# Two additions moved from VectorE to TensorE and ScalarE, and TensorE's ration counted anew, in a Mamba and linear-attention kernel

## The chip, the cores and the metric

The kernel runs on one core of a Trainium2 chip. The metric is the device time of one execution in microseconds (us), as the median of several runs. A profile of one execution comes with it. The engines are named PE or TensorE (matrix products; PEld is its loading of weights), DVE or VectorE, ACT or ScalarE, POOL or GpSimd, and SP, which here only issues DMAs. Each engine takes its instructions in the order in which they were written to it.

## The reference

The input x has 4 batches of 512 channels on 64 x 64 places; flattened, 4096 time steps. Two layers follow each other, and each adds its input to its output.

```python
# layer 0: x = x + L0(group_norm(x))
xn = layer_norm(xf)                                  # over the 512 channels
chunks = xn in 4 chunks of 128 channels, each a sequence of its own
xz = chunks @ in_proj_w.T;  xi, z = split(xz)        # 256 channels each
xc = silu(conv4(xi) + conv_b)                        # causal, 4 taps, by channel
dt, Bs, Cs = xc @ x_proj_w.T;  dt = softplus(dt @ dt_proj_w.T + dt_proj_b)
h = exp(dt * A) * h + (dt * xc) * B                  # 16 states for each channel
y = sum over states of h * C;  y = (y + xc * D_param) * silu(z)
ym = y @ out_proj_w.T + skip_scale * chunks          # the skip addition
out = layer_norm(ym) @ proj_w.T + proj_b             # then x + out: the input addition
# layer 1: x = x + L1(group_norm(x)): linear attention, 8 heads, ReLU on q and k,
# then an output projection
```

## The kernel before

**Tiles and steps.** Time is cut into 8 tiles of 512. A step is one chunk (128 channels) of one tile of one batch: 4 x 8 x 4 = 128 steps, c innermost. Each step's recurrence takes 16 slots. A slot holds two scans of 128 x 512 on VectorE (`slot`, L582, the scan at L596), where the partitions are 32 channels times 4 states. Around the scans stand: the decay exp(dt A) on ScalarE into one of two PSUM buffers (`decay`, L565), dt x B on GpSimd (`drive`, L574), two slots ahead into three buffers, the product with C (`product`, L614), whose first 384 columns are VectorE's, from a bank c_all that TensorE spreads (`c_row`, L559), and whose last 128 columns are GpSimd's (L607), and the sum over the states, on TensorE with the constant `fold` (`fold_states`, L625). The matrix `fold` is four 32 x 32 identities under each other.

**What else runs in the slots.** The function `after` (L971) is called at the end of each slot and hands out the rest of the work at fixed slots s of the step: gate on GpSimd (s = 1 and 9), the softplus of the next step (s = 2), the output product of the step before (`out_proj`, L647, s = 3) and its skip addition on VectorE (`with_skip`, L652, s = 5), the inputs of the step after next (`inputs`, L440), Silu (s = 10), and so on. At s = 2 and 10 (`AWAY`) ScalarE is away with table loads.

**The queues of generators.** Four lists hold work that is handed out piece by piece: `ahead` (group norm and layer norm of the next tile), `late` (`projected`, L409: the second layer norm, the projection and the input addition of a finished tile), `rest` (`attention`, L668, of the batch before) and `light` (`stats0`, L656: the statistics of the next batch, two pieces of VectorE work for a tile of x at the AWAY slots). A piece that yields "wait" is tried again. `later(n, what)` puts an instruction off by n slots, so that its operands are there. `work_bank` takes one of four PSUM banks; `load` takes one of three tiles of x and issues its DMA on SP.

**The ration.** `mm` (L117) counts each product in `work["mm"]`, in units of a 128 x 512 fp32 product (a quarter for bf16; for products that run abreast, their share). In each slot, a credit of 2.5 units less what `after` itself issued decides whether a queue may issue products:

```python
credit = min(credit + 2.5 - (work["mm"] - start), 2.5)
```

Here `start` is taken at the top of `after`, so the products of `fold_states` and `c_row`, which `slot` issues before it, are not counted.

**The end.** The attention of a batch needs the whole batch's first layer. That of batches 0 to 2 runs in the slots of the next batch; that of batch 3 runs after the last scan, with no recurrence beside it.

Of the kernel before, what the change touches and what calls it, by code (L numbers as in the profile page):

```python
# [11 lines left out]
ALU = mybir.AluOpType  # L12
# [12 lines left out]
def kernel(  # L25
# [53 lines left out]
    def work_bank(name, behind=1):  # L79
        held[0] += behind  # L80
        return ps_w.tile([P, T], F32, tag="w", name=name)

    def free(n=1):
        held[0] -= n
# [15 lines left out]
    def until(*done):  # L100
        while not all(done):
            yield "wait"
# [92 lines left out]
    def column(v, n, name):  # L195
        t = const.tile([P, n], F32, tag=name, name=name)
        nc.scalar.dma_start(t, v.rearrange("(c p) -> p c", p=P))
        return t

    def rows(v, t, queue=nc.scalar):  # L200
        queue.dma_start(t, v.rearrange("(c p) f -> p c f", p=P))
        return t
# [39 lines left out]
        nc.vector.tensor_scalar(dg[:, e, :], ident, dpar[:, e : e + 1], None, ALU.mult)  # L242
    g_sb = column(norm_g, NC, "g_sb")
    b_sb = column(norm_b, NC, "b_sb")
    a_sb = rows(a_log, wk.tile([P, NH, NST], F32, tag="sq", name="a_sb", bufs=4))
    w_op = const_rows(op_w, "w_op")
    sk = const.tile([P, 1], F32, tag="sk", name="sk")
# [22 lines left out]
    for k in range(KS):  # L270
        for j in range(NJ):
            nc.sync.dma_start(
                a_t[k * BLK : (k + 1) * BLK, :, j, :], a_k[j * BLK : (j + 1) * BLK, :, k, :]
            )

    for o in range(NC):
        pw = work_bank(f"pw_{o}")
# [131 lines left out]
    def projected(ym, stats, x1, b, t):  # L409

        nm = f"{b}_{t}"
        yield from layer_norm(ym, f"b_{nm}", False)
        xt = yield from load_x(b, t, "r")
        taken = []

        def take(o, pp):
            nc.vector.scalar_tensor_tensor(  # L417
                xt[:, o, :], pp, pb[:, o : o + 1], xt[:, o, :], ALU.add, ALU.add
            )
            nc.vector.bn_stats(stats[:, o, t, :], xt[:, o, :])  # L420
            free()

        for o in range(NC):
            yield from room()
            pp = work_bank(f"pp_{nm}_{o}")
            for c in range(NC):
                mm(
                    pp, w_pr[:, c, o * P : (o + 1) * P], ym[:, c, :],
                    start=(c == 0), stop=(c == NC - 1),
                )  # L430
                if c == 1:
                    yield "more"
            taken.append(later(2, lambda o=o, pp=pp: take(o, pp)))
            yield
        yield from until(*taken)
        nc.sync.dma_start(x1, xt)
        later(2, free_x)

# [205 lines left out]
            f["xz"][:, 1, e, :], f["xz"][:, 1, e, :], f["xz"][:, 0, e, :], ALU.mult  # L644
        )

    def out_proj(f, nm):  # L647
        f["po"] = work_bank(f"po_{nm}", 0)
        for e in range(NH):
            mm(f["po"], w_op[:, e, :], f["xz"][:, 1, e, :], start=(e == 0), stop=(e == NH - 1))  # L650

    def with_skip(f, xn, c):  # L652
        v = xn[:, c, NTAP - 1 : NTAP - 1 + T]
        nc.vector.scalar_tensor_tensor(v, v, sk, f["po"], ALU.mult, ALU.add)

    def stats0(stats, b):  # L656

        for t in range(NT):
            xt = yield from load_x(b, t, "s")
            yield  # L660
            for c in range(NC):
                nc.vector.bn_stats(stats[:, c, t, :], xt[:, c, :])
                if c == NC - 1:
                    later(1, free_x)
                if c % 2:
                    yield

    def attention(b, x1s, stats):  # L668

# [165 lines left out]
        free_x()  # L835
        free_x()
        for o in range(NC):
            r = slice(o * P, (o + 1) * P)
            nc.vector.tensor_tensor(m3[:, o, r], m3[:, o, r], ident, ALU.add)
        def store(t, o, pp):  # L840
            res = wk.tile([P, T], F32, tag="res", name=f"res_{b}_{t}_{o}", bufs=1)
            nc.scalar.activation(res, pp, AF.Identity, bias=ob[:, o : o + 1])
# [112 lines left out]
        decay(k)  # L955

    with tc.manual_schedule():
        credit, mix, held[0], held_x[0] = 0.0, iter(()), 0, 0
        for n, (b, t, c) in enumerate(steps):
            f, nm = fs[n], names[n]  # L960
            before = fs[n - 1] if n else None
            nxt = fs[n + 1] if n + 1 < N else None
            front = step_inputs(n + 2) if n + 2 < N else iter(())
            last_mix, mix = mix, mixers(fs[n + 2], names[n + 2]) if n + 2 < N else iter(())
            if c == 0 and (t + 1 < NT or b + 1 < B):
                add_to(ahead, tile_norm(b, t + 1) if t + 1 < NT else tile_norm(b + 1, 0))
            if c == 0 and t == 0 and b + 1 < B:
                add_to(light, input_norm(b + 1))
            assert c != 2 or not ahead
            for s in range(SLOTS):  # L970
                def after():  # L971
                    nonlocal credit
                    start = work["mm"]
                    now[0] = n * SLOTS + s
                    for what in [w for at, w in due if at <= now[0]]:
                        what()
                    due[:] = [d for d in due if d[0] > now[0]]
                    if s == 0 and before is not None:
                        take_y(before, n - 1, 1)
                    if s == SLOTS // 2:  # L980
                        take_y(f, n, 0)
                    if s < 2:
                        next(last_mix, None)
                    if s == 1:
                        spread(f, 1, nm)
                        if before is not None:
                            gate(before, 1)
                        if nxt is not None:
                            time_banks(nxt, names[n + 1])
                    if s == 2 and nxt is not None:  # L990
                        nc.scalar.preload_act_table_set("softplus")
                        time_steps(nxt, names[n + 1])
                        nc.scalar.preload_act_table_set("natural_log_exp_and_others")
                    if s == 5 and before is not None:
                        pb_, pt_, pc_ = steps[n - 1]
                        with_skip(before, xn[pb_, pt_], pc_)
                        if pc_ == NC - 1:
                            add_to(late, leave(pb_, pt_))
                    if s in (2, 4, 5, 6, 7, 8):
                        next(front, None)  # L1000
                    if s == 3 and nxt is not None:
                        to_rows(nxt, 0, names[n + 1])
                        to_rows(nxt, 1, names[n + 1])
                    if s == 3 and before is not None:
                        out_proj(before, names[n - 1])
                    if s == 9:
                        gate(f, 0)
                        if nxt is not None:
                            spread(nxt, 0, names[n + 1])
                    if s == 10 and n + 2 < N:  # L1010
                        silu(n + 2)
                        nc.scalar.preload_act_table_set("natural_log_exp_and_others")
                    if s >= 12:
                        next(mix, None)
                    may = [
                        what for k, what in ((0, "wide"), (1, "one ahead"), (2, "two ahead"))
                        if any(a - 2 * k <= s <= a - k for a in AWAY) or (k == 2 and s >= SLOTS - 2)
                    ]
                    if s in AWAY and not any(q and q[0][1] == "wide" for q in (ahead, late)):
                        one(light)  # L1020

                    limit[0] = 3 if 9 <= s < 13 else 2
                    credit = min(credit + 2.5 - (work["mm"] - start), 2.5)
                    busy = False
                    for queue in (ahead, late, rest):
                        kind = queue[0][1] if queue else None
                        if queue is ahead or kind == "free" or credit > 0 or kind == "more" and not busy:
                            start = work["mm"]
                            one(queue, ANYWHERE if queue is ahead and (c, s) > (1, 4) else may)
                            credit -= work["mm"] - start  # L1030
                            busy = busy or work["mm"] - start > 1

                slot(n * SLOTS + s, N * SLOTS, after)
            fs[n - 1].clear() if n else None
        product(N * SLOTS - 1, N * SLOTS)
        now[0] = None
        for _, what in due:
            what()
    take_y(fs[N - 1], N - 1, 1)
    gate(fs[N - 1], 1)  # L1040
    out_proj(fs[N - 1], names[N - 1])
    with_skip(fs[N - 1], xn[B - 1, NT - 1], NC - 1)
    add_to(late, leave(B - 1, NT - 1))
    while late or rest:
# [54 lines left out]
```

## Time and profile before

| | us |
|---|---|
| median of 3 runs | 8307.17 (8304.55 to 8308.64) |
| the profiled execution | 8301.55 |
| its span | 8299.8 |
| first scan, end of the last product of the recurrence | 122.8, 7845.5 |
| busy: VectorE, GpSimd, TensorE, ScalarE | 7350.8, 6856.9, 6564.5, 5235.9 |
| DMA | 153 GB/s on average |

A group of the profile is read so: the line of the kernel, the engine, the operation, the tile written and the tiles read with their shapes, the count; then the busy time and the mean duration in ns; then the idle time of the engine just before these instructions and what ended it. A row of the waits reads: who waited, for whom, us in total, how many times, the longest. Every product on TensorE has line 120, that of the helper `mm`, so there one goes by the names of the tiles: po is the output product, pp the projection, pq, pk and pr the attention's products, y the sum over the states, pc the taps. A product of fp32 operands leaves two records.

### The profile page before, as it was taken

To read this page: it belongs to the slowest core of one execution; us is meant where nothing else is said; L and a number is where in the kernel's file an instruction comes from. 1 tells how busy PE (TensorE), PEld (TensorE's weight loads), DVE (VectorE), ACT (ScalarE), POOL (GpSimd) and SP (SyncE) were. 2 spreads that over 40 slices of the span, in tenths; PEclk is the share of its full clock that TensorE was granted. 3 is DMA by queue.
4 is the path that set the end of the run, shared out by engine and by line. 5 is a ranking of instruction groups with operands and counts; after the bars stand their busy time and mean duration, and the time that the engine had idled before them with its cause. 6 is when DMAs were issued, how large, how long until landed. Compare 5 with 4: busy or idle time off the path is not lost. (4 is left out here: it accounts for less than half of the span.)

```text
span 8299.8 us, 86977 instructions
## 1 busy us (share of the span) xinstructions
PE 6564.5 (79%) x22240; PEld 2203.5 (27%) x22240; DVE 7350.8 (89%) x7097; ACT 5235.9 (63%) x7585; POOL 6856.9 (83%) x4565
## 2 busy tenths in 40 slices
PE   5667676667788878788788888788788888888699
PEld 1111121112222222222222222223222222232244
DVE  5999999999999999989999999999999999999700
ACT  4666666666666666666677666666666666666421
POOL 4999999999888888888898888888988888888600
PEclk8787888777889989899898999889889999889799
DMA  5666666556666565666666666657666655666412
GB/s 158 160 157 153 152 158 151 146 143 158 161 161 154 144 162 148 159 180 172 168 152 159 161 154 160 154 151 190 161 160 157 152 147 144 154 168 177 128 41 86
DMA packets 829306, 1266.15 MB, mean 153 GB/s; under 512 B 183920, under 2 KB 317568, under 8 KB 816512
## 3 DMA queue, kind: packets, MB, share of 16 engines
q1 hardware_dynamic: 821632, 1255.87, 59.6%
q10 hardware_dynamic: 7168, 4.71, 0.2%
q8 instruction: 174, 2.85, 0.2%
q14 instruction: 332, 2.72, 0.1%
HBM read 1053.28 MB, written 206.57 MB: 152 GB/s over the span
## 5 line engine op out<-in xcount | busy, mean ns | idle before, releaser
L578 POOL TENSOR_TENSOR bx<-d_all,b_all 128x1024 f32<-128x1024 f32 x2048 | 4795.3, 2362 | 107.3 <-DVE h L596 90.4
L596 DVE TENSOR_TENSOR_SCAN h<-dA,st,bx 128x512 f32<-128x512 f32 x3584 | 4448.5, 1272 | 228.2 <-ACT dA L570 182.8
L570 ACT ACTIVATE dA<-d_all,a_t 128x512 f32<-128x512 f32 x4096 | 2805.3, 689 | 2473.2 <-DVE h L596 2450.5
L619 DVE TENSOR_TENSOR h<-h,c_all 128x768 f32<-128x768 f32 x2048 | 1913.7, 934 | 91.3 <-PE c_all L120 81.3
L120 PE MATMUL y<-h,fold 128*32 128x512 f32 x8192 | 1329.7, 727 | 128.2 <-POOL h L607 121.9
L120 PE MATMUL c_all<-parts,sel 128*128 128x384 bf16 x1024 | 379.6, 371 | 1316.0 <-DVE h L619 1313.4
L607 POOL TENSOR_TENSOR h<-h,c_sb 128x512 f32<-128x512 f32 x1024 | 1298.9, 1268 | 129.8 <-DMA c_sb<-c_rows 28.5
L120 PE MATMUL pq<-w_qk,xa 128*128 128x512 f32 x2048 | 1038.9, 639 | 1.1 <-ACT xa L321 1.1
L120 PE MATMUL pc<-xn,w_cv 128*128 128x512 f32 x2048 | 1026.8, 631 | 11.3 <-ACT xn L389 4.6
L606 POOL COPY st<-h 128x4 f32<-128x4 f32 x1024 | 193.3, 189 | 640.4 <-DVE h L596 580.0
L120 PEld LDWEIGHTS <-sel 128*128 128x128 bf16 x1280 | 128.1, 100 | 2133.0 <-DVE h L619 1933.8
L596 DVE TENSOR_TENSOR_SCAN h<-dA,bx 128x512 f32<-128x512 f32 x512 | 604.2, 1211 | 87.0 <-ACT dA L570 83.4
L120 PEld LDWEIGHTS pc<-xn,w_cv 128*128 128x128 f32 x2048 | 382.3, 199 | 674.3 <-issue 559.7
L120 PEld LDWEIGHTS pq<-w_qk,xa 128*128 128x128 f32 x2048 | 413.1, 206 | 491.1 <-issue 471.7
L120 PE MATMUL pp<-xn,w_pr 128*128 128x512 f32 x1024 | 523.9, 642 | 3.8 <-DVE xn L383 3.8
L120 PE MATMUL pr<-xb,m 128*128 128x512 f32 x1024 | 514.9, 641 | 2.7 <-ACT xz L469 2.3
L120 PE MATMUL pt<-dt,w_dt 32*128 32x512 f32 x512 | 276.0, 879 | 116.7 <-ACT parts L525 50.6
L120 PE MATMUL y<-xz,dg 128*128 128x512 f32 x512 | 347.9, 769 | 0.0
L120 PEld LDWEIGHTS y<-h,fold 128*32 128x32 f32 x8192 | 172.4, 116 | 651.3 <-issue 310.8
L643 POOL TENSOR_TENSOR xz<-xz 128x512 f32<-128x512 f32 x256 | 325.3, 1271 | 2.7 <-ACT xz L640 2.7
L488 POOL TENSOR_TENSOR dt<-dt,xz 128x1024 f32<-128x1024 f32 x128 | 302.8, 2366 | 20.5 <-ACT dt L481 20.5
L120 PE MATMUL pd<-xz,w_xp 128*128 128x512 f32 x512 | 297.0, 710 | 7.8 <-ACT xz L911 7.8
(151 smaller groups left out, 5871.3 us busy)
## 6 DMA issues: line engine op xcount, KB each, us to landing
d_all<-d_rows SPq DMA_DIRECT2D x2048, 256.0 KB, 6.5
b_all<-b_rows SPq DMA_DIRECT2D x4096, 64.0 KB, 2.1
d_rows<-dt SPq DMA_DIRECT2D x256, 512.0 KB, 3.0
c_sb<-c_rows SPq DMA_DIRECT2D x4096, 16.0 KB, 1.8
xs<-in_x_dram SPq DMA_DIRECT2D x32, 1024.0 KB, 7.3
xn<-in_x_dram SPq DMA_DIRECT2D x32, 1024.0 KB, 6.1
xr<-in_x_dram SPq DMA_DIRECT2D x32, 1024.0 KB, 6.4
x<-xr SPq DMA_DIRECT2D x32, 1024.0 KB, 4.0
```

The costliest lines, as they stand in the source:

```text
L120: nc.tensor.matmul(out_, lhsT, rhs, **how)
L488: nc.gpsimd.tensor_tensor(f["both"][:, 1], f["both"][:, 0], f["xz"][:, 0], ALU.mult)
L570: nc.scalar.activation(dAs[k], fs[n]["d_all", e][:, 0, j, :], AF.Exp, scale=a_t[:, e, j, q : q + 1])
L578: nc.gpsimd.tensor_tensor(bxs[g], fs[n]["d_all", e][:, 1, jj * 2 : jj * 2 + 2, :], bc(b_all[g // JJ], 2), ALU.mult)
L596: nc.vector.tensor_tensor_scan(h[:, j, :], dAs.pop(2 * g + i), bxs[g][:, i, :], 0.0 if t == 0 else st[:, c, e, q, j : j + 1], ALU.mult, AL ...
L606: nc.gpsimd.tensor_copy(st[:, c, e, q, :], h[:, :, T - 1])
L607: nc.gpsimd.tensor_tensor(h[:, :, CUT:], h[:, :, CUT:], bc(c_sb.pop(g // JJ), NJ), ALU.mult)
L619: nc.vector.tensor_tensor(own, own, bc(c_all[g // JJ], 2), ALU.mult)
L643: nc.gpsimd.tensor_tensor(f["xz"][:, 1, e, :], f["xz"][:, 1, e, :], f["xz"][:, 0, e, :], ALU.mult)
```

## The change

The skip addition becomes a product: `out_proj` first multiplies the chunk with `skd`, a diagonal matrix of the skip scale, into the bank po, and the two products of the output projection are added to it there. `with_skip` is then a copy from the bank, on ScalarE. The input addition becomes four products of 32 x 32 blocks of `fold` with the tile xr, added to the bank pp; ScalarE takes the bank out with the bias, and the statistics of the result (`bn_stats`) follow one slot later, as does the store. `skd` takes the place of `ident` in memory, so that the later addition of the identity to m3 goes by blocks of `fold`. A tile of `stats0` is loaded in the slot after the last tile's work, not at the next AWAY slot. The credit is now 3.5 units a slot, at most 2.6, and `seen` makes it count all products since the last slot, those of the recurrence too.

```diff
+    skd = ident
...
+    nc.vector.tensor_scalar(skd, ident, sk, None, ALU.mult)
...
         def take(o, pp):
-            nc.vector.scalar_tensor_tensor(
-                xt[:, o, :], pp, pb[:, o : o + 1], xt[:, o, :], ALU.add, ALU.add
-            )
-            nc.vector.bn_stats(stats[:, o, t, :], xt[:, o, :])
+            nc.scalar.activation(xt[:, o, :], pp, AF.Identity, bias=pb[:, o : o + 1])
             free()
+            later(1, lambda: nc.vector.bn_stats(stats[:, o, t, :], xt[:, o, :]))
...
                 mm(
                     pp, w_pr[:, c, o * P : (o + 1) * P], ym[:, c, :],
-                    start=(c == 0), stop=(c == NC - 1),
+                    start=(c == 0), stop=False,
                 )
                 if c == 1:
                     yield "more"
+            for k in range(P // BLK):
+                r = slice(k * BLK, (k + 1) * BLK)
+                mm(pp[r, :], fold[r, :], xt[r, o, :], abreast=P // BLK, start=False, stop=True)
             taken.append(later(2, lambda o=o, pp=pp: take(o, pp)))
             yield
         yield from until(*taken)
+        yield from pause(1)
         nc.sync.dma_start(x1, xt)
...
-    def out_proj(f, nm):
-        f["po"] = work_bank(f"po_{nm}", 0)
+    def out_proj(f, xn, c, nm):
+        po = f["po"] = work_bank(f"po_{nm}", 0)
+        mm(po, skd, xn[:, c, NTAP - 1 : NTAP - 1 + T], start=True, stop=False)
         for e in range(NH):
-            mm(f["po"], w_op[:, e, :], f["xz"][:, 1, e, :], start=(e == 0), stop=(e == NH - 1))
+            mm(po, w_op[:, e, :], f["xz"][:, 1, e, :], start=False, stop=(e == NH - 1))
...
-        v = xn[:, c, NTAP - 1 : NTAP - 1 + T]
-        nc.vector.scalar_tensor_tensor(v, v, sk, f["po"], ALU.mult, ALU.add)
+        nc.scalar.copy(xn[:, c, NTAP - 1 : NTAP - 1 + T], f["po"])
...
-                    yield
+                    yield "wait" if c == NC - 1 else None
...
         for o in range(NC):
-            r = slice(o * P, (o + 1) * P)
-            nc.vector.tensor_tensor(m3[:, o, r], m3[:, o, r], ident, ALU.add)
+            for k in range(P // BLK):
+                r = slice(k * BLK, (k + 1) * BLK)
+                v = m3[r, o, o * P + k * BLK : o * P + (k + 1) * BLK]
+                nc.vector.tensor_tensor(v, v, fold[r, :], ALU.add)
...
-                    start = work["mm"]
...
-                    if s in AWAY and not any(q and q[0][1] == "wide" for q in (ahead, late)):
+                    if light and light[0][1] == "wait" or s in AWAY and not any(
+                        q and q[0][1] == "wide" for q in (ahead, late)
+                    ):
                         one(light)
...
-                    credit = min(credit + 2.5 - (work["mm"] - start), 2.5)
+                    credit = min(credit + 3.5 - (work["mm"] - seen), 2.6)
...
+                    seen = work["mm"]
```

More of the change, by code (lines that the diff above doesn't have):

```diff
@@ L957 @@
     with tc.manual_schedule():
-        credit, mix, held[0], held_x[0] = 0.0, iter(()), 0, 0
+        credit, seen, mix, held[0], held_x[0] = 0.0, work["mm"], iter(()), 0, 0
         for n, (b, t, c) in enumerate(steps):
@@ L971, in after @@
                 def after():
-                    nonlocal credit
-                    start = work["mm"]
+                    nonlocal credit, seen
                     now[0] = n * SLOTS + s
@@ L1004, in after @@
                     if s == 3 and before is not None:
-                        out_proj(before, names[n - 1])
+                        pb_, pt_, pc_ = steps[n - 1]
+                        out_proj(before, xn[pb_, pt_], pc_, names[n - 1])
                     if s == 9:
@@ L1040 @@
     gate(fs[N - 1], 1)
-    out_proj(fs[N - 1], names[N - 1])
+    out_proj(fs[N - 1], xn[B - 1, NT - 1], NC - 1, names[N - 1])
     with_skip(fs[N - 1], xn[B - 1, NT - 1], NC - 1)
```

## The prediction

> **What bounds the kernel now.** I read the busy line first, then the costliest groups, then the stretches of the span, then the waits of VectorE, and last the chain of waits for the end.
>
> ```profile
> PE 6564.5 (79%) x22240; PEld 2203.5 (27%) x22240; DVE 7350.8 (89%) x7097; ACT 5235.9 (63%) x7585; POOL 6856.9 (83%) x4565
> ...
> L596 DVE TENSOR_TENSOR_SCAN h<-dA,st,bx 128x512 f32<-128x512 f32 x3584 | 4448.5, 1272 | 228.2 <-ACT dA L570 182.8
> ...
> L619 DVE TENSOR_TENSOR h<-h,c_all 128x768 f32<-128x768 f32 x2048 | 1913.7, 934 | 91.3 <-PE c_all L120 81.3
> ```
>
> VectorE leads, with two scans and one product in each slot (2 x 1.272 + 0.934 = 3.48 us). The share over the whole span hides that there are two stages. The rows of the stretches show them (each engine: busy us, then its instructions in brackets; after POOL the granted clock):
>
> ```profile
> 200.00:2110.00 1910.00, 1324.09 (x4155) 370.35 (x4156) 1844.81 (x1740) 1258.38 (x1803) 1755.04 (x1169) 0.79 0.62 153
> 2110.00:4020.00 1910.00, 1557.37 (x5434) 530.21 (x5432) 1784.60 (x1717) 1265.57 (x1838) 1661.76 (x1106) 0.91 0.63 161
> ...
> 7900.00:8300.00 400.00, 392.98 (x1436) 183.32 (x1434) 16.86 (x45) 83.03 (x129) 0.00 (x0) 0.98 0.17 61
> ```
>
> The recurrence runs from the first scan at 122.8 to the end of the last at 7844.5: 7722 us, 128 steps of 16 slots, 3.77 us a slot. In batch 0 (first row) VectorE is busy 97% of the time; once the attention of the batch before runs beside it (second row) 93%, with TensorE at 82%. In all it idles 437 us of the 7640 between 200 and 7840. The last row is the tail: the last batch's attention, TensorE alone at 98%. The chain of waits holds nearly only this tail (PE pq, pr), so it says nothing of the stage in which the change lies. What VectorE waits for:
>
> ```profile
> DVE h L596 <- ACT dA L570: 266.3, 178, 49.1
> ...
> DVE h L619 <- PE c_all L120: 81.3, 63, 3.0
> ...
> DVE xn L654 <- PE po L120: 16.8, 16, 6.8
> DVE xr L417 <- PE pp L120: 15.8, 8, 6.4
> ```
>
> The first comes at ScalarE's table loads and Silu, which the change leaves alone. The second is TensorE's queue running late. All 63 of those waits lie where attention runs, none in batch 0.
>
> **What the Trainium skill says.** "VectorE: DVE Perf Modes", Specifications, puts VectorE closer to SBUF and ScalarE closer to PSUM; here ScalarE's copy of a 128x512 bank takes 0.578 us (L469) and VectorE's addition out of one 0.729 us (L654), which agrees. "TensorE: Matmul & The Clock Gate", Part 1, says that idling throttles the clock and activity releases it; the granted clock is 0.79 in batch 0 and 0.91 with attention, so added products should not slow the others. Part 3 of that page says products on distinct row groups of the array run abreast; two K=32 products (pt, four records) took 1.13 us together at 2469.40, as long as one full product. It also says that matmuls start and end in order. So a product that waits for a DMA holds all behind it.
>
> **The change, part by part.**
>
> *VectorE's work removed.* The rows are:
>
> ```profile
> L417 DVE SCALAR_TENSOR_TENSOR xr<-pp,pb,xr 128x512 f32<-128x512 f32 x128 | 94.0, 735 | 48.5 <-PE pp L120 15.8 <-DMA b_all<-b_rows 14.6 <-DMA xr<-in_x_dram 12.1
> L654 DVE SCALAR_TENSOR_TENSOR xn<-xn,sk,po 128x512 f32<-128x512 f32 x128 | 93.3, 729 | 17.3 <-PE po L120 16.8
> ```
>
> 127 of the L654 lie in the recurrence (the last step's is in the tail) and 124 of the L417 (the last tile's four are in the tail): 127 x 0.729 + 124 x 0.735 = 183.7 us, on an engine 94% busy: **-184**.
>
> *Waits of VectorE removed.* Idle before those rows was 17.3 and 48.5; in the tail 6.8 and 11.0; so 48 us in the recurrence. What they waited for (products, and xr landing) is still waited for, by ScalarE and TensorE. I take half as gained: **-24** (0 to -48).
>
> *ScalarE's pieces.* 127 copies (0.58) and 124 Identity with a bias (0.68, as L842): 158 us on an engine 63% busy, with no table load (Identity already stands among the Exp at L453). What can suffer is the decay (L570) queued behind a piece. In the timeline ScalarE idles alternately 0.48 and 1.35 us before each decay, and a decay takes 0.69 where the next scan takes 1.28 before it is needed. So a piece in the short gap makes the decay some 0.2 late, inside that slack; two pieces together, or one beside a table load, cost. I take 0.1 each: **+25** (0 to +158). A piece also holds the queue when TensorE is late with its bank: that was VectorE's wait above.
>
> *TensorE's products.* Each step gets a skip product (po: 260.8 us for 256 products of two records, 1.02 each) and each tile four groups of four 32x32 products abreast; the like group (y, eight records) runs in 1.06 when nothing holds it. 128 x 1.02 + 128 x 1.06 = 266 us more on an engine that has 18% free beside attention. Cost comes through c_all: its product stands behind the slot's other products, and VectorE waits. I counted the products between one c_all and the next in the order of both programs (in units of a 128x512 fp32 product; bf16 and 32-wide ones a quarter). A unit takes 0.86 when dense (two products every 1.72 us at 3036.85), 0.94 at a clock of 0.91, so a pair of slots (7.54 us) holds about 8. Pairs over 8 units: 163 before, 229 after. The c_all waits (81.3 before L619, 6.6 before L596) times 229/163 give **+36** (-30, if the evener ration spreads them, to +200, priced below).
>
> *The fold products wait for the load of xr.* In batch 0 they stand one slot behind it:
>
> ```profile
> 475.56 1.01 SPq L130 DMA_DIRECT2D xr<-in_x_dram  x1
> ...
> 479.09 1.88 PE L120 MATMUL pp<-xn,w_pr 128*128 128x512 f32 x4
> ...
> 483.81 0.75 DVE L417 SCALAR_TENSOR_TENSOR xr<-pp,pb,xr 128x512 f32<-128x512 f32 x1 [2.18 <-DMA xr<-in_x_dram]
> ```
>
> TensorE would stand from 480.97 to about 483.8, some 2.8 us, with two tap products (pc, 1.72) and the next c_all behind it: 483.8 + 1.06 + 1.72 + 0.32 = 486.9, where VectorE wants it at 486.39. VectorE lost 2.18 to this load before, so this is an exchange, and I count nothing more. In batches 1 to 3 most tiles have about three slots (11 us) between their first product and the fold in the written-out order; the longest landing was 11.8. If that cover goes, it is 2.8 x 31 tiles = 87 on TensorE.
>
> *GpSimd.* It idles 869 us between 200 and 7840, 6.8 a step; VectorE gets 1.44 a step faster (183.7/128). Most of GpSimd's waits are for the scan, and its bursts (gate, dt) must be caught up in less time: **+15** (0 to +92).
>
> *The ration.* Limit 3.5 with the recurrence's own work (0.72 units a slot: 1.0 fold, 0.19 c_all, a quarter of 1.0 for y, per pair) is 2.78 for the rest against 2.5. The order of the changed program shows what that yields: the attentions' last products stand at steps 64.7, 96.7 and 126.75 of 128, before at 64.4, 96.4 and 126.9. None spills into the tail, so **0** of itself (its spreading is in the -30 above).
>
> *The rest.* The earlier loads of xs move DMAs on SP's queue by some slots; the bn_stats behind them are as many, at the same slots: 0, and if a tile is then short the attention would end late, which the order excludes. The store of xr goes one slot later; it is read a batch later: 0. The 16 additions of ident (0.785) become 64 of 32x32, near the fold copies' 0.172 (L188): 12.6 against 11.0, 0. The extra scaling of ident is 0.28 at the start. The tail gets one skip product and four groups in its serial part: **+5** (3 to 8).
>
> Sum: -184 - 24 + 25 + 36 + 15 + 5 = **-127**. The profiled execution took 8301.55 (span 8299.8): 8174.6. The median of the runs, 8307.17, is 5.6 above it, so **8180**.
>
> **The rivals.**
>
> *TensorE becomes the bound (slower).* With attention beside it, every added product passes on to c_all and to VectorE: 96 steps x (1.02 + 1.06) = 200 in place of 36, so -184 - 24 + 25 + 200 + 15 + 5 = +37: 8344. It decides where VectorE's waits for c_all go from 88 to over 88 + 163 = 251. For: 82% busy, 20 waits a batch already, pairs over 10 units 54 before and 82 after. Against: the mean pair goes only from 6.0 to 6.2 units, and every pair below 8 catches up what one above it left. 0.14.
>
> *ScalarE's pieces land in full.* 158 in place of 25: +6, 8313, no change. For: the decay is what VectorE waits for most. Against: those waits cluster at table loads, and pieces like L453 run now without a wait beside them. 0.08.
>
> *GpSimd takes over half.* It gives back 92: -50, 8257. For: 89% busy in the recurrence. Against: VectorE waits only 11 us for it now (bx, h, st). 0.10.
>
> *The change does not do what it says.* The ration might be all that acts; the order above speaks against it, and the removed rows are gone from VectorE's order.
>
> **How the numbers follow.** The forecast has 0.68, its own range is 8095 (-212: waits all gone, ScalarE's pieces free, c_all no worse) to 8260 (about 60 for ScalarE's pieces and 70 for c_all). With the rivals the range goes to 8315, which leaves out the slower case (0.14) and about 0.05 below. 0.2%, 17 us, is about what a measurement of this kernel can tell from no change: faster 0.68 + 0.10 = 0.78, same 0.08, slower 0.14.
>
> **What would show it.** Right: VectorE busy near 7164, its idle between 200 and the last scan near 490 (437 - 24 + 25 + 36 + 15), c_all waits near 125, no VectorE row for po or pp; TensorE busy near 6830; the tail 5 longer. Wrong: c_all waits above 250, waits for dA grown by over 100, GpSimd's idle unchanged while VectorE's grows, or po or fold rows well over 1.1 us a group.

## The result, and the profile after

The changed kernel takes 8273.33 us (median of 4 runs, 8265.77 to 8280.80) against 8305.86 (4 runs, 8303.44 to 8308.64) for the kernel before on the same chip: a ratio of 0.9961, 95% interval 0.9943 to 0.9978. It gains 33 us, 0.4%, where 127 were forecast. The direction was right, the size was not: the range held the time, but the likeliest value is 93 us off. The profiled execution took 8270.61 us, with a span of 8268.9. The granted clock hardly differs: where attention runs it is 0.92 (0.91 before).

The page's busy line and the two groups that carry the recurrence:

```profile
PE 6698.2 (81%) x23450; PEld 2248.1 (27%) x23520; DVE 7187.9 (87%) x6890; ACT 5366.3 (65%) x7841; POOL 6856.1 (83%) x4565
...
L602 DVE TENSOR_TENSOR_SCAN h<-dA,st,bx 128x512 f32<-128x512 f32 x3584 | 4432.6, 1269 | 236.4 <-ACT dA L576 141.8
...
L625 DVE TENSOR_TENSOR h<-h,c_all 128x768 f32<-128x768 f32 x2048 | 1909.2, 932 | 256.0 <-PE c_all L120 246.1
```

VectorE has 163 us less to do (7350.8 before), so the work did leave it. The time did not follow: the idle time before the product with c_all went from 91.3 to 256.0. The stretches say where (busy us and instructions of PE, PEld, DVE, ACT, POOL; then the clock, the DMA share, GB/s):

```profile
200.00:2110.00 1910.00, 1367.55 (x4485) 384.14 (x4484) 1815.62 (x1690) 1296.92 (x1874) 1769.22 (x1178) 0.80 0.63 154
2110.00:4020.00 1910.00, 1597.09 (x5754) 542.77 (x5770) 1759.87 (x1679) 1308.99 (x1916) 1674.25 (x1114) 0.92 0.64 162
...
7880.00:8268.00 388.00, 381.41 (x1375) 179.73 (x1387) 18.23 (x56) 77.53 (x120) 0.00 (x0) 0.97 0.18 63
```

In batch 0 VectorE is busy 95% (97% before), beside attention 92% (93%). TensorE is at 84% there (82%). The last row is the tail, with TensorE alone at 98% as before. The last product of the recurrence starts at 7807.0 (7844.5 before), so the recurrence gained 37.5; from there to the end it is 461.9 (455.3), which gives back 6.6.

What VectorE waits for:

```profile
DVE h L625 <- PE c_all L120: 246.1, 114, 11.2
...
DVE h L602 <- ACT dA L576: 226.2, 172, 49.1
DVE h L602 <- issue: 55.0, 37, 3.2
DVE h L602 <- POOL h L613: 25.1, 25, 2.4
```

The waits for c_all are three times as long in all (81.3 before), and the longest single one is 11.2 (3.0 before). Batch by batch they are 23.5, 71.9, 77.8 and 72.8; before 0, 27.4, 25.8 and 28.2. So they grew in batch 0 too, where no attention runs. The waits for the decay and those without a named cause come to 281.2 (266.3 + 18.0 = 284.3 before), so no harm of ScalarE's new pieces is to be seen here. Those for GpSimd grew from about 11 to 41.

The groups of the new work (TensorE and ScalarE; the bank `po` is multiplied with `skd`, which is the tile of ident), and the additions of `fold` to m, which took the place of L839:

```profile
L120 PE MATMUL po<-xn,ident 128*128 128x512 f32 x256 | 146.4, 654 | 0.0
...
L120 PE MATMUL pp<-xr,fold 32*32 32x512 f32 x1024 | 140.2, 618 | 31.9 <-DMA xr<-in_x_dram 31.8
...
L421 ACT ACTIVATE xr<-pp,pb 128x512 f32<-128x512 f32 x128 | 86.8, 678 | 64.2 <-PE pp L120 63.4
...
L847 DVE TENSOR_TENSOR m<-m,fold 32x32 f32<-32x32 f32 x64 | 19.4, 304 | 23.4 <-PE pob L120 22.6
```

146.4 / 128 is 1.14 us for a skip product, 140.2 / 128 is 1.10 for a group of fold products: near the 1.02 and 1.06 of the forecast. The 31.9 is the first surprise. TensorE stands before the fold products until the load of xr lands, 14 times, 31.8 us in all. (The row of its weight loads shows 46.8 us of waits for the same landing, in 18 places; the 14 are among them, so the two do not add up.) The worst place, in the timeline:

```profile
3838.78 2.62 PE L120 MATMUL pp<-xn,w_pr 128*128 128x512 f32 x4
...
3845.12 0.40 SPq L130 DMA_DIRECT2D xr<-in_x_dram  x1
...
3851.99 1.93 PE L120 MATMUL pp<-xr,fold 32*32 32x512 f32 x8 [7.15 <-DMA xr<-in_x_dram]
...
3853.85 3.61 PE L120 MATMUL pr<-xb,m 128*128 128x512 f32 x4
...
3857.30 0.33 PE L120 MATMUL c_all<-parts,sel 128*128 128x384 bf16 x1
...
3857.66 0.95 DVE L625 TENSOR_TENSOR h<-h,c_all 128x768 f32<-128x768 f32 x1 [11.19 <-PE c_all L120]
```

SP issues the load at 3845.12, 6.3 us after the first product of this bank has started, and it lands just before 3851.99. TensorE waits 7.15 for it with the attention's products (pr, 3.61) and the next c_all behind it in its queue, and VectorE, which needs nothing of xr, stands for 11.19.

### The profile page after: what moved, and what is told of

It is laid out like the page before. It is cut to its first block, busy times and chain, and to the rows that moved or that the text cites. A ratio compares the mean times of both kernels' runs of the same rounds, so it can differ in the third digit from the quotient of the medians.

```text
span 8268.9 us, 89639 instructions
## 1 busy us (share of the span) xinstructions
PE 6698.2 (81%) x23450; PEld 2248.1 (27%) x23520; DVE 7187.9 (87%) x6890; ACT 5366.3 (65%) x7841; POOL 6856.1 (83%) x4565
## 5 line engine op out<-in xcount | busy, mean ns | idle before, releaser
L625 DVE TENSOR_TENSOR h<-h,c_all 128x768 f32<-128x768 f32 x2048 | 1909.2, 932 | 256.0 <-PE c_all L120 246.1
L120 PE MATMUL y<-h,fold 128*32 128x512 f32 x8192 | 1278.2, 700 | 122.7 <-POOL h L613 118.7
L120 PE MATMUL c_all<-parts,sel 128*128 128x384 bf16 x1024 | 374.2, 365 | 1097.2 <-DVE h L625 1094.7
## 6 DMA issues: line engine op xcount, KB each, us to landing
d_all<-d_rows SPq DMA_DIRECT2D x2048, 256.0 KB, 6.6
```

Source lines behind the costliest of these rows:

```text
L120: nc.tensor.matmul(out_, lhsT, rhs, **how)
L625: nc.vector.tensor_tensor(own, own, bc(c_all[g // JJ], 2), ALU.mult)
```

## Experiments

The theory after the result was that two costs ate the gain, both by way of the place of c_all in TensorE's queue: the wait for the landing of xr, and the mere volume of the added products. The rivals were ScalarE's pieces in front of the decay, the new count in the ration, and a saving on VectorE that was small from the start. Ratios are to the kernel before, with 95% intervals that reach 5 to 15 us to either side; where two medians differ by less than some 15 us, the text says that they are not told apart.

### The ration

The changed kernel with the ration of before:

```diff
-                    credit = min(credit + 3.5 - (work["mm"] - seen), 2.6)
+                    credit = min(credit + 2.5 - (work["mm"] - start), 2.5)
```

> The changed kernel with the ration of before (2.5 units a slot, the recurrence's own products not counted). Theory Q (the added products in TensorE's in-order queue delay c_all, wherever the ration puts the rest): c_all waits fall only a little from 246 us, to 190 to 240, and 23 of the last attention product's 128 steps spill behind the last scan (some 20 us in the tail), so 8260 to 8295. Theory R (the new ration packs the attention's products into worse places): c_all waits fall to 90 to 130 and the time, with the spill, to 8150 to 8180. Theory L (the fold products wait for the landing of xr and hold the queue): c_all unchanged, 8290.

It took 8264.7 us (ratio 0.9947, 0.9933 to 0.9960), by the intervals not told apart from the changed kernel. Inside it two things offset each other. VectorE's waits for c_all fall to 175.5, and the recurrence's last product starts 27 us sooner (7780.2). But 23 of the 128 products pr of the last attention that runs in the slots (batch 2's) had not been let out by then, and from there to the end it takes 473.9 instead of 461.9. And the other way round, the kernel before with the new ration alone:

> The kernel before with the new ration alone (3.5 units a slot with the recurrence's products counted, at most 2.6); its attention ends some 4 steps of 128 earlier in each batch. Theory Q: c_all waits stay near those of before (81 us), 80 to 120, and the time within 8300 to 8340. Theory R: c_all waits of 180 to 250 and 8400 to 8470. Theory L says nothing: 8306, no change.

8299.7 us (0.9990, 0.9982 to 0.9998), with 100.0 of waits for c_all. So the ration is not what gained. That it can cost the recurrence time once the products are there is seen in the 27 us; it comes up again below, with the load ahead.

### All but the products

The changed kernel without the skip and fold products, everything else in place (the count in the ration included):

```diff
-            for k in range(P // BLK):
...
-                mm(pp[r, :], fold[r, :], xt[r, o, :], abreast=P // BLK, start=False, stop=True)
+            work["mm"] += 1.0
...
-        mm(po, skd, xn[:, c, NTAP - 1 : NTAP - 1 + T], start=True, stop=False)
+        work["mm"] += 1.0
```

> The changed kernel without the skip and fold products themselves (so the skip and the input are not added); the ration counts them as if they were there, so that all other instructions keep their order, and ScalarE takes the banks out as in the changed kernel. Theory Q: the c_all waits go back to 70 to 110 us and the time falls by 130 to 170, to 8100 to 8145. Theory R: c_all waits stay above 170, time 8210 to 8250. Theory L: the fold's part alone goes, c_all near 180, time near 8210. If ScalarE's pieces were what took the gain, the time would stay at 8250 or more.

8163.9 us (0.9828, 0.9814 to 0.9841). VectorE's waits in it:

```profile
DVE h L600 <- ACT dA L574: 230.5, 181, 49.6
DVE h L623 <- PE c_all L120: 129.6, 94, 4.2
DVE h L600 <- issue: 51.6, 33, 3.0
```

Taking the additions off VectorE is worth 144 us, with ScalarE's 251 pieces and the smaller parts of the change (the earlier loads of `stats0`, the later store) in place, and with the waits for the decay (230.5 + 51.6) no longer than before. The added products cost 8273.3 - 8163.9 = 109. That drops ScalarE as a rival, and a small saving on VectorE too. It also shows that c_all is waited for more (129.6 against 81.3) even without a product added. A VectorE that comes back to it sooner would do this, but the count in the ration has a part: the new one alone, on the kernel before, had raised these waits to 100.0.

### The landing of xr

Two experiments take that wait away. In the first, the fold products read another tile that is already there, ym:

```diff
-                mm(pp[r, :], fold[r, :], xt[r, o, :], abreast=P // BLK, start=False, stop=True)
+                mm(pp[r, :], fold[r, :], ym[r, o, :], abreast=P // BLK, start=False, stop=True)
```

> The changed kernel with the fold products reading the normed tile, which is there long before, in place of the just loaded xr (so the input addition adds another tensor); order and number of all instructions are the same. Theory L: TensorE's 78 us of waiting for xr go, c_all waits fall to about 180 and the time by 50 to 70, to 8205 to 8225. Theories Q and R: the time falls by no more than 25, to 8250 to 8270, and c_all waits stay above 220.

In the second, the load gets two slots of lead before the generator goes on:

```diff
+        yield from pause(2)
```

> The changed kernel, right in all it computes, with two slots of pause between the load of xr and the projection's first product, so that the tile has landed when the fold products come. If the landing cost 39 us in the changed kernel as the exchange of the operand says: 8225 to 8245, no wait of TensorE for xr. If the pause only moves the wait elsewhere (the tiles of x are held longer, the attention starts later): 8260 to 8280.

They took 8234.3 (0.9912, 0.9899 to 0.9926) and 8236.4 us (0.9910, 0.9897 to 0.9924). The wait costs 37 to 39 us by the medians, and one line takes it away. (The 78 us of waiting in the first expectation count each stop twice, once at the weight load; the products stood 31.8.) In the kernel with the load ahead, the group of the fold products and VectorE's wait read:

```profile
L120 PE MATMUL pp<-xr,fold 32*32 32x512 f32 x1024 | 137.4, 606 | 0.0
```

```profile
DVE h L603 <- ACT dA L577: 230.8, 162, 49.3
DVE h L626 <- PE c_all L120: 194.3, 105, 4.2
```

The idle time before the group is 0.0, and the longest wait for c_all is 4.2. But 194.3 of such waits remain, 65 more than without the products (129.6), and 8236.4 - 8163.9 = 72 us of the time: the volume. (The kernel without the products has no pause, so the pause itself is in the 72.)

### One addition at a time

With the input addition back on VectorE and only the skip addition a product:

> The changed kernel with the input addition back on VectorE (no fold products; the ration counts them still, so the order of all else stays). From 8273: VectorE gets 124 x 0.64 = 79 us of work back and the fold's products (the landing, 39 us, and their volume) go. Theory V (volume alone matters, so skip and fold products, as many and as long, cost 35 us each beside the landing): 8273 + 79 - 39 - 35 = 8278, c_all waits near 170. Theory S (the skip product costs nearly all of the 70 us, since it stands in the densest pair of slots): 8273 + 79 - 39 = 8313 or more, c_all waits near 200. Theory F (the fold costs it all): 8273 + 79 - 109 = 8243, c_all near 130.

8258.5 us (0.9935, 0.9923 to 0.9947). With the skip addition back on VectorE and only the input addition a product:

> The changed kernel with the skip addition back on VectorE (no skip product; the ration counts it still). From 8273: VectorE gets 127 x 0.64 = 81 us back. Theory V: 8273 + 81 - 35 = 8319, c_all near 210. Theory S: 8273 + 81 - 70 = 8284, c_all near 180. Theory F: 8273 + 81 = 8354, c_all near 245.

8294.9 us (0.9982, 0.9974 to 0.9990). Neither time is one of the three that were set for it. Each half alone gains less than VectorE's work in it, the skip addition 49 us of some 80 and the input addition 13. The input half brings the wait for xr with it (35.9 us at the products), which is one reason why it is the poorer; taking that half away makes the changed kernel quicker by 15, at the edge of what the intervals tell apart.

### More of the suspected volume

Each skip product issued a second time, not counted in the ration (128 more products):

```diff
+        mm(po, skd, xn[:, c, NTAP - 1 : NTAP - 1 + T], start=False, stop=False)
+        work["mm"] -= 1.0
```

> The changed kernel with the skip product issued twice in each step (so the skip is added twice); the second is not counted in the ration, so all else keeps its order. If a product at s = 3 costs what taking the skip product out and putting VectorE's addition back suggests (about 59 us for 128): 8310 to 8335, c_all waits near 300. If the added products cost only as far as they fill slack once: 8273 to 8290. If their cost rises with what is there already: above 8345.

8319.3 us (1.0013, 1.0007 to 1.0020), 46 more than the changed kernel. VectorE's wait:

```profile
DVE h L625 <- PE c_all L120: 279.0, 130, 10.5
```

46 / 128 is 0.36 us for a product that takes 1.02 to 1.14 on TensorE. So about a third of an added product reaches the end here, though TensorE is idle a fifth of the span. TensorE's own waits suggest why that idle time does not absorb it:

```profile
PE c_all L120 <- DVE h L625: 1094.7, 505, 10.4
...
PE pp L120 <- DMA xr<-in_x_dram: 31.8, 14, 7.2
```

Most of it, 1094.7 us (1313.4 before), is TensorE waiting in front of c_all, whose pool has one buffer, until VectorE has read the old one. Then VectorE has two scans, about 2.5 us, before it needs the new one. By this reading TensorE cannot work ahead of that place and may not be late at it: a light pair of slots turns into waiting, a heavy one is passed on. The test would be a second buffer for c_all, filled a pair sooner; it was not made, so the single buffer is argued as the reason and not shown.

### The best version, and what the ration is worth with it

The load ahead and the old manner of counting, at 2.65 units a slot (at 2.5, products had spilled into the tail):

```diff
+        yield from pause(2)
...
-                    credit = min(credit + 3.5 - (work["mm"] - seen), 2.6)
+                    credit = min(credit + 2.65 - (work["mm"] - start), 2.65)
```

> As e7_load_ahead, and the ration counted as before (only what the slot's own call issued), but with 2.65 units a slot, which makes up for the 0.125 that the added products take and lets the last attention end before the last scan. If the new count costs the recurrence 27 us, as the old one's run says (its recurrence ended 27 us sooner, and its tail was longer by the spilled products): 8195 to 8215. If that came from the fewer units and not from the count: 8225 to 8245.

8206.1 us (0.9874, 0.9859 to 0.9889): by the medians 67 us under the changed kernel and 101 under the kernel before, the best that was run.

```profile
DVE h L603 <- ACT dA L577: 307.8, 194, 51.4
...
DVE h L626 <- PE c_all L120: 123.7, 104, 3.6
```

The waits for c_all are at 123.7; those for the decay take up some of it (307.8 + 13.7 without a cause, 281.2 in the changed kernel). The same without the two products:

> As e8_load_ahead_old_count without the skip and fold products (so the skip and the input are not added; the ration counts them as if they were there). It shows what the products still cost where the load has landed and the ration is of the old count. Theory Q with volume alone: as much as the 70 us that they cost under the new count (8234 less 8164), so 8136. If the old count has taken most of that cost away too: 8165 to 8195.

8175.5 us (0.9840, 0.9827 to 0.9854). Here the products cost 31, against 72 under the new count with the load ahead; without the products the old manner and the new one (8163.9) are not told apart. So the price of a product is no constant: 31 / 256 = 0.12 us in this order, 72 / 256 = 0.28 in that.

Since a count of heavy pairs had served in the forecast, it was tried as a guide: the skip product one slot sooner (s = 2), which leaves 46 instead of 75 pairs of slots over 10 units.

> As e8_load_ahead_old_count, with the skip product issued one slot sooner (s = 2, the emptiest slot of that part of the step, in place of s = 3, the fullest); the two other products into the same bank stay at s = 3. In the written-out order the pairs of slots over 10 units between two c_all fall from 75 to 46. Theory Q (what counts is the work between two c_all products): c_all waits fall from 124 us to 90 to 110 and the time by 10 to 30, to 8175 to 8196. If the place within the step does not matter, only the volume: 8200 to 8212. If the bank held one slot longer starts a wait for banks: 8220 or more.

8215.7 us (0.9891, 0.9878 to 0.9905), with 152.6 of waits for c_all: not better, though the count fell. The wait for a free bank that the expectation names is not the reason. TensorE stands 21.6 us before po for that (res 17.9, kq 3.7), but in the kernel with s = 3 it stands as long before the tap products pc (16.8 and 6.6): the stop has only moved.

What made the old count better with the load ahead: the manner of counting, or the rate at which attention's products are let out? Four more kernels, all with the load ahead:

> The changed kernel with the load ahead of the input's products and the old manner of counting, but with the rate raised from 2.65 to 2.78 units a slot and the cap lowered to 2.6, so that the attention's products are spent about as early as under the new count (its plan ends a batch's attention near slot 63.2, 95.2 and 125.1, against 64.7, 96.7 and 127.1 for the load ahead with the old count at 2.65). If it is the manner of counting that made the old count 30 us quicker with the load ahead, this takes about 8206 us, with VectorE waiting some 125 us for c_all. If it is the rate (products that are spent a slot or two later overall, or that spill into the tail), it takes about 8236 us, with some 190 us of waits for c_all. In between, both have a part.

> The changed kernel with the load ahead, and the new count's limit at 3.45 in place of 3.5, with which the planned attention ends at steps 64.69 and 96.66 as in the kernel with the old count at 2.65 (with 3.5: 64.25 and 96.25). If it is where the attention's products end that matters, about 8206 us, with some 125 us of waits for c_all. If it is the manner of counting, 8236 us and some 190. By the order, the units over 7.5 between two products of c_all come to 453 for this one, 455 for the limit of 3.5 and 426 for the old count at 2.65, which speaks for 8236.

> The same with the new count's limit at 3.37, which is 2.65 and the 0.72 units that the recurrence itself has in a mean slot, so the mean rate of the old count at 2.65; the cap on what is saved up is 3.6 in place of 2.6. If it is the rate alone, about 8206 us; if it is the manner of counting, about 8236. The units over 7.5 between two products of c_all come to 432 (426 for the old count at 2.65), which speaks for about 8210.

> The kernel with the load ahead and the old count at 2.6 in place of 2.65 (with the cap at 2.65). From 2.78 to 2.65 the time fell by 65 us. If the rate is what counts and it goes on, 8180 to 8200 us; if the plan at 2.65 already spreads the attention over the whole batch (it ends at steps 64.69 and 96.66, here at 64.91 and 96.91), nothing more is to be had: about 8206, or some more where products run late into the tail.

| count | rate, cap | us (ratio, 95% interval) | waits for c_all |
|---|---|---|---|
| old | 2.60, 2.65 | 8220.2 (0.9894, 0.9881 to 0.9908) | 141.2 |
| old | 2.65, 2.65 | 8206.1 (0.9874, 0.9859 to 0.9889) | 123.7 |
| old | 2.78, 2.6 | 8271.5 (0.9956, 0.9942 to 0.9970) | 227.5 |
| new | 3.37, 3.6 | 8269.0 (0.9955, 0.9941 to 0.9968) | 192.1 |
| new | 3.45, 2.6 | 8235.8 (0.9915, 0.9901 to 0.9928) | 179.9 |
| new | 3.50, 2.6 | 8236.4 (0.9910, 0.9897 to 0.9924) | 194.3 |

Two of the four, at 2.78 and 3.37, came out where no expectation had put them. Neither answer holds alone. The new count at the old one's mean rate (3.37) is 63 slower than that one, so it is not the rate alone; the cap differs too (3.6), and it was not varied by itself. The old count spans the whole field, 8206 to 8272, so it is not the manner alone. (The first two rows are hardly told apart, the last two not at all.) Where the planned attention ends is no answer either: at 3.45 and at 2.65 it is the same step. The units over 7.5 between two products of c_all missed as well: 432 were counted for the one with 8269.0, 426 for the one with 8206.1. What stays open is which property of the order makes it good. Nor need it be TensorE's order alone, for the ration also moves the work of VectorE and ScalarE that hangs on the products: VectorE's waits for the decay run from 230.8 to 336.8 in these six. What is shown: with the same instructions, the order in which the ration hands them out is worth up to 65 us here, twice what the change gained.

## Why the direction came out right and the size did not

By the runs the change falls into two parts. Without the added products the forecast's terms come to -184 - 24 + 25 + 15 = -168; measured were -144. The products were put at 36, with 5 more for the tail; they cost 109. So some 24 of the 93 us lie with the other terms, VectorE's work above all, and 68 with the products: with the wait for xr, which was put at nothing, and with the volume, which was priced at half.

**What bounds the kernel: right.** VectorE's queue with the recurrence, and c_all as the wait through which TensorE is felt. The tail grew by 6.6 (5 forecast) and VectorE's busy time is 7187.9 (7164).

**VectorE's work removed, -184: too large by some 17.** Busy time from 200 to the recurrence's end fell from 7208.0 to 7046.5, by 161, with the additions of `fold` taking 6 more than those of ident in that stretch. The step added durations of records, but records of neighbours overlap. The timeline of the kernel before, at a skip addition:

```profile
477.67 0.72 DVE L654 SCALAR_TENSOR_TENSOR xn<-xn,sk,po 128x512 f32<-128x512 f32 x1
478.31 1.28 DVE L596 TENSOR_TENSOR_SCAN h<-dA,st,bx 128x512 f32<-128x512 f32 x1
```

The next instruction starts 0.64 after it, not 0.72. The Trainium skill ("Perfetto Trace Analysis", Optimizing Scalar/DVE Operations) says that a part of the profiled latency, the acknowledgement of the write, overlaps with the next instruction, which agrees. The price of an instruction on a full queue is the distance of starts.

**The load of xr, 0: the first step that failed.** The forecast called TensorE's wait for xr an exchange for VectorE's, on the one place in batch 0, and for the other batches trusted three slots (11 us) of cover between a bank's first product and the fold. In the trace of the changed kernel those two lie only 4.5 to 9.1 us apart in batches 1 to 3 (the standing left out), where the load takes 6.1 at the median from issue to landing; and at the three longest stops (7.15, 6.88, 4.36) SP issued it 4.9 to 6.4 us after the first product had started. So the cover was not there. The place in batch 0 that had been worked out at 2.8 measured 0.90. In all TensorE stands 31.8 us before these products, less than the 87 that the forecast set for a loss of the cover, and the runs put the effect at 37 to 39. It is no exchange since the two queues are not alike. VectorE's wait for xr delayed VectorE alone, by 12.1 in all; TensorE's holds the attention's products and the next c_all with it, and VectorE pays for what stands behind the stop too (after the one of 7.15 it waited 11.19). That products start and end in order (the Trainium skill, "TensorE: Matmul & The Clock Gate", Part 3) was cited in the forecast, with the very consequence, and the timeline of the worst place agrees. What was missing was to apply it to every tile, with the time at which SP issues its load.

**TensorE's volume through c_all, +36: the second step that failed, half of what it cost in this order.** Waits for c_all went from 87.9 (81.3 + 6.6) to 246.1, by 158. Of the rise at the product itself (165), the kernel without the added products shows 48, which the forecast did not have at all; the rest, 117, is the products, 52 of it gone with the load ahead and 65 left. In time the volume is 72. The step's method, the ratio of the counts of heavy pairs, could not have told this: the later orders had like counts and other times. In the best order the volume costs 31, about what was forecast, but nothing in the count picked that order out, so that near agreement is luck.

**ScalarE's pieces, +25: none found.** Waits for the decay and unnamed ones stayed (284.3 to 281.2), without the products too (282.1). The 0.578 and 0.729 us that the forecast set beside each other are a plain copy and an addition of two tiles, so they do not tell by themselves which engine lies nearer to PSUM. **GpSimd, +15:** its waits grew by 30, within the bounds given. **The ration, 0:** right for itself (the kernel before with it alone is 0.999 of before), but with the products and the load ahead its settings span 65 us.

**TensorE busy near 6830: 6698.2.** The products account for 210 (6488.5 without them, with 70 of the records missing in the changed one), not 266; the rest of the kernel shows 76 less than before, and why stays open.

The measured terms make -161 (VectorE) - 48 (waits of the removed rows) + 158 (c_all) - 3 (ScalarE) + 30 (GpSimd) + 7 (tail) = -17, where the span fell by 31; 14 us of small waits and overlaps stay unassigned. By the runs, which are surer than that sum: everything but the products gained 144, and the products took 109 back, 37 to 39 at the load and the rest by volume. The rival "TensorE becomes the bound" had the mechanism: with 158 for 36, the forecast's own sum is -5. Its point of decision, 251, was nearly reached (246.1). By this sum a gain was left because ScalarE's 25 were not paid and all of the 48 us of waits went instead of half, so the right direction is in part luck. (The upper end of the forecast's own range, 8260, lies 11 above what the terms named for it give: -184 - 24 + 60 + 70 + 15 + 5 = -58, or 8249. Nothing rests on it.)

## What to carry to other kernels

Before work is moved to an engine that executes in order, list what each moved instruction waits for and what stands behind it: a wait on a DMA that harmed one consumer becomes a wait of the whole queue, and here two slots of lead for the load were worth 37 us. Idle time of an engine that itself waits for the bottleneck (here for VectorE to free c_all) need not be room to fill. And where an added product cost between 0.12 and 0.36 us, by the order around it and by what else stood there, try several orders before the change is judged: the best here gained three times what the first did.

## What was not expected of the hardware

Cutting the additions of the identity to m into blocks cost time, though only a quarter of the elements was left: 19.4 us for the 64 of 32 x 32 (L847) against 11.9 for the 16 of 128 x 128 (L839). The means, 304 and 785 ns, mislead here. The shortest, the median and the longest of each, in ns:

```profile
L839 DVE TENSOR_TENSOR m<-m,ident x16: 277/289/2428, 3528.1 to 8183.4; 128x128 f32<-128x128 f32 x16
```

```profile
L847 DVE TENSOR_TENSOR m<-m,fold x64: 168/183/2322, 3493.1 to 8154.0; 32x32 f32<-32x32 f32 x64
```

So the price of a block is 183, near the 172 of the copy from which it was forecast, and the price of a whole addition is 289 and not the mean of 785: four blocks cost more than the one addition that they replaced. The long ones are few, five in each kernel (1.35 to 2.43 us before, 0.58 to 2.32 after), and all ten have one thing in common. While VectorE stands in them, GpSimd is at an instruction that VectorE's addition has nothing to do with, mostly bx, and the addition ends 0.04 to 0.15 us after GpSimd's does. In the kernel after:

```profile
3491.93 4.67 POOL L584 TENSOR_TENSOR bx<-d_all,b_all 128x1024 f32<-128x1024 f32 x2
...
3493.14 6.25 DVE L847 TENSOR_TENSOR m<-m,fold 32x32 f32<-32x32 f32 x16
```

The first two of these 16 additions take 3.5 us, up to 3496.64, where bx ends at 3496.60; the other 14 take 2.8 in all. Three additions that had begun when GpSimd's instruction started took their usual time, and in the tail, where GpSimd does nothing, no block took longer than 0.19. That GpSimd holds VectorE up in such an addition is the reading that fits all ten; no run tested it.
